# Every product as two of 64 stationary columns, in a linear-attention and expert kernel on one Trainium2 core

## The chip, the cores and the metric

The kernel runs on one core of one Trainium2 chip. The metric is the device time of one execution in microseconds (us). All data are float32. "TensorE" (PE in the profile) multiplies matrices, "PEld" is its loading of weights (the stationary operand), VectorE is DVE, ScalarE is ACT, GpSimd is POOL, and SyncE (SP) issues most of the DMAs.

## The reference

A layer norm, then linear attention with a decay per head and a gate, and beside it a linear layer with eight low-rank experts of which each token uses two; both are added to the input.

```python
BATCH, SEQ, HIDDEN = (2, 512, 512); HEADS, HEAD_DIM = (32, 128)
xn = layernorm(x)
qkv = silu(xn @ qkv_w.T)                       # 3 * 32 heads * 128
...                                             # per head, in blocks, with decay:
scores = einsum('bhnd,bhmd->bhnm', cq, ck) * diag_decay
intra  = einsum('bhnm,bhmd->bhnd', scores, cv)
inter  = einsum('bhnd,bhde->bhne', cq * q_decay, kv)
kv_next = kv * block_decay + einsum('bhnd,bhne->bhde', ck * k_decay, cv)
...
xf = attn * rsqrt(mean(attn * attn) + EPS)
gate = sigmoid(xn @ gate_w.T)
attn_out = gate * (norm_w * xf) @ out_w.T
...
probs = softmax(xn @ W_router.T); top 2 of 8, renormalised -> combine
h  = einsum('nd,erd->ner', xn, A) * combine[:, :, None]
ffn_out = xn @ W_base.T + b_base + einsum('ner,eor->no', h, B) * 2
return x + attn_out + ffn_out
```

## The kernel before

**Products.** A product is one call of `nc.tensor.matmul(o, lhsT, rhs)`: `lhsT` is the stationary operand (128 rows by up to 128 columns), `rhs` the moving one (128 rows by N columns), `o` a tile in PSUM with as many partitions as `lhsT` has columns. In float32 the compiler makes of each call two weight loads and two matrix instructions, one after the other: load, matmul, load, matmul. N is 256 in the projections, in the base linear layer and in the output projection, 128 in the attention, 512 in the experts' product and 136 in the router's. The code makes 3048 products: 2072 with N = 256, 936 with N = 128 (40 of them are products of the identity by itself, which fill two banks, and transposes), 32 with N = 136 and 8 with N = 512.

**Stages.** (1) The tokens (8 tiles of 128) are normalised, transposed on TensorE (`transpose`, L264) and used by the router's product (`router`, through `mm`, L90) and by the base linear layer (`base`, L314), which is split by a scheme of Strassen's kind into seven products of half size; the base product is spread among the transposes by hand (`AFTER`). (2) The projections to q, k, v and the gates: two levels of the same scheme, so 49 small products instead of 64. GpSimd makes the sums of weights (`encode`: tiles `s` and `e`), VectorE the sums of tokens (`xsum`, `xt`), and `inner_product` (L431 and L434) makes the products into banks named `ps_fr`, `ps_sc` and `sd`. ScalarE and VectorE combine the results (`after`: L503, L506, L519, L521, L527, L538). (3) The attention of one head and batch (`attend`): scores (`ps_sc<-qk`), state updates (`ps_sc<-v,kd`) and results (`ps_at`), all through `mm` (L90). k is brought into another layout by DMA through HBM (`k_kept`, `kt`). Its steps are placed among the slots of the projection loop. (4) The output projection, 16 pairs of heads for each of two halves of the tokens, again by seven products (`out_product`, L806), with sums made by VectorE (`gsum`) and GpSimd (`wsum`).

**Order.** From the transposes to the first output products the order on every engine is that of the code (`tc.manual_schedule`); one loop over slots of one inner product each (`SLOTS`, `later`, `stages`) interleaves projections, attention and DMAs. The rest of the output projection, after `in_order.close()` (L965), is ordered by the framework's scheduler. Accumulation: most products write with `start` on the first use of a bank only and with `skip_group_check=True`, so one bank holds several running sums.

`mm` (L89) is the helper through which the router, the attention and the experts go; `base`, `inner_product` and `out_product` call `nc.tensor.matmul` themselves.

Of the kernel before, what the change touches and what calls it, by code (L numbers as in the profile page):

```python
# [42 lines left out]
P = 128  # L43
# [7 lines left out]
NP = H // 2  # L51
# [10 lines left out]
def attn_moe_kernel(ctx: ExitStack, tc: tile.TileContext, x, qk_w, v_w, gate_w, out_w, norm_w,  # L62
                    decay, base_w, base_b, router_a_w, lora_b, out):
    nc = tc.nc
# [15 lines left out]
    def bank(tag):  # L80
        return ps.tile([P, 512], F32, tag=tag, name=f"ps_{tag}", bufs=banks[tag])
# [3 lines left out]
    def ring(tag, shape=None):  # L85
        n, bufs = RING[tag]
        return work.tile(shape or [P, n * 512], F32, tag=tag, name=tag, bufs=bufs)

    def mm(o, lhsT, rhs, start, stop):  # L89
        nc.tensor.matmul(o, lhsT, rhs, start=start, stop=stop)  # L90

    ssq = [keep.tile([P, S], F32, tag=f"ssq{b}", name=f"ssq{b}") for b in range(B)]
    ident = keep.tile([P, P], F32, tag="ident", name="ident")
# [18 lines left out]
    def inv_sqrt(mean_sq, y, z):  # L112

        nc.vector.reciprocal(y, z)
        nc.vector.scalar_tensor_tensor(z, mean_sq, EPS, y, ALU.add, ALU.mult)
        nc.vector.scalar_tensor_tensor(z, z, -0.5, y, ALU.mult, ALU.mult)
        nc.vector.scalar_tensor_tensor(y, z, 1.5, y, ALU.add, ALU.mult)
        return y
# [10 lines left out]
    def kind(n):  # L129
        return 2 if n >= VG else n % 2  # L130
# [60 lines left out]
    for n in range(NSET):  # L191

        start = {0: [(0, 1), (1, 1), (0, 6)], 1: [(0, 4), (1, 6)]}.get(n, [(n, 1), (n - 1, 4), (n, 6)])
# [11 lines left out]
    with tc.tile_pool(name="setup", bufs=1, side="right") as sp:  # L205
# [26 lines left out]
        def tokens(t, c):  # L232

            b, tt = divmod(t, TB)
            of = slice(tt * P, (tt + 1) * P)
            return xnT[:, c, of] if b == 0 else b12[:, c, of] if c < 2 else b22[:, c - 2, of]
# [8 lines left out]
        def statistics(t):  # L245
            if t:
                nc.vector.bn_stats(stats[:, t, :], x_sb[t])
                nc.vector.bn_aggr(mv[:, t, :], stats[:, t, :])
            else:
                both = sp.tile([P, 2, 6], F32, tag="both", name="both")  # L250
                for i, of in enumerate(halves):
                    nc.vector.bn_stats(both[:, i, :], x_sb[0][:, of])
                nc.vector.bn_aggr(mv[:, 0, :], both)
            for g, ts in enumerate(groups):
                if t == ts[-1]:
                    roots[g] = root(sp, mv[:, ts[0] : t + 1, 1], len(ts), f"ln{g}")
# [15 lines left out]
        def router(t):  # L272
            ra = bank("sc")
            for c in range(KC):
                mm(ra[:, : NE + ER], tokens(t, c), wra[:, c, :], c == 0, c == KC - 1)
            nc.scalar.copy(ra_sb[:, t, :], ra[:, : NE + ER])
# [3 lines left out]
        HO = HID // 2  # L280
# [3 lines left out]
        wo = dict(zip(range(1, 8), (a11, a12, wsums[3], a22, wsums[0], wsums[1], wsums[2])))  # L284
        xo = dict(zip(range(1, 8), (b11, b21, b22, xsum[3], xsum[0], xsum[1], xsum[2])))

        def base():

            pa, pb = seeded[:2], first_banks
            pc, pd, y, w = {}, {}, {}, {}  # L290

            def done(b, half, h, o):
                nc.sync.dma_start(x_base[:, TB * b + 2 * h : TB * b + 2 * h + 2, half * HO : (half + 1) * HO],
                                  o.rearrange("p (t n) -> p t n", t=2))

            def copied(tag, t):
                o = ring(tag, [P, 512])
                nc.scalar.copy(o, t)
                return o

            def added(t, u):
                o = ring("scores")
                nc.vector.tensor_tensor(o, t, u, ALU.add)
                return o


            units = [(1, 0, 0), (1, 0, 1), (2, 0, 0), (2, 0, 1), (1, 1, 0), (1, 1, 1), (2, 1, 0), (2, 1, 1)]
            for q, h, i in units + [(q, h, i) for q in (5, 6, 7, 3, 4) for h in range(2) for i in range(2)]:
                if q == 5 and i == 0:
                    pc[h] = bank("sc")  # L310
                t = {1: pa, 2: pa, 5: pc, 3: pc, 6: pb, 7: pd, 4: pd}[q][h]
                of = slice((2 * h + i) * P, (2 * h + i + 1) * P)
                for c in range(2):
                    nc.tensor.matmul(t[:, i * HO : (i + 1) * HO], xo[q][:, c, of], wo[q][:, c, :],  # L314
                                     start=q in (1, 5) and i == 0 and c == 0, stop=True, skip_group_check=True)
                if i == 0:
                    pass
                elif q == 1:
                    nc.scalar.copy(pb[h], t)
                elif q == 2:  # L320
                    done(0, 0, h, copied("scores", t))
                elif q == 5:
                    y[h] = copied("gT", t)
                elif q == 6:
                    pd[h] = pa[h]
                    nc.scalar.copy(pd[h], t)
                    w[h] = copied("gate", t)
                elif q == 7:
                    done(1, 1, h, added(t, y[h]))
                elif q == 3:  # L330
                    done(1, 0, h, added(t, w[h]))
                else:
                    done(0, 1, h, copied("scores", t))
                yield

        chunks = base()

        first_banks = [seeded[2], bank("at")]  # L340
# [10 lines left out]
        for g, ts in enumerate(groups):  # L351
            rstd = inv_sqrt(*roots[g])
            xns = []
            for i, t in enumerate(ts):
                xn = ring("gate")
                for of in halves if t == 0 else (slice(0, HID),):
                    (nc.vector if t < NT - 1 else nc.gpsimd).tensor_scalar(
                        xn[:, of], x_sb[t][:, of], mv[:, t, 0:1], rstd[:, i : i + 1], ALU.subtract, ALU.mult)
                xns.append(xn)

            for t in range(2 * g, 2 * g + 2) if 0 < g < 4 else ():
                statistics(t)
            for t, xn in zip(ts, xns):
                transpose(t, xn)
                for what in AFTER[t]:
                    if what == "base":
                        next(chunks)
                    else:
                        router(what)
        nc.vector.tensor_tensor(wsums[0], a21, a22, ALU.add)  # L370
        nc.vector.tensor_tensor(wsums[1], wsums[0], a11, ALU.subtract)
        nc.vector.tensor_tensor(wsums[2], a11, a21, ALU.subtract)
# [15 lines left out]
        HB = S // 2  # L388
# [34 lines left out]
    def inner_product(o, r, i, first):  # L423
        n, q = rounds[r]
        a = operand[n, q][i]
        x_ = {1: xo[q][:, 0, :HB], 2: xo[q][:, 1, :HB], 3: xo[q][:, 1, HB:], 4: xt[q - 1][:, 3],
              5: xt[q - 1][:, 0], 6: xt[q - 1][:, 1], 7: xt[q - 1][:, 2]}[i]
        for u in range(2):
            if kind(n) == 0:

                nc.tensor.matmul(o.rearrange("p (g j d) -> p j g d", g=2, j=2)[:, u], x_[:, u * P : (u + 1) * P],  # L431
                                 a, start=first and u == 0, stop=True, skip_group_check=True)
            else:
                nc.tensor.matmul(o[:, u * HB : (u + 1) * HB], a[:, u], x_, start=first and u == 0, stop=True,  # L434
                                 skip_group_check=True)

# [215 lines left out]
    def attend(head, b):  # L654
# [22 lines left out]
        for j in range(TB):  # L677
            mm(pc[:, j * P : (j + 1) * P], k[:, j * P : (j + 1) * P], q[:, j * P : (j + 1) * P], True, True)
# [77 lines left out]
    HT, HO = S // 2, HID // 2  # L756
# [37 lines left out]
    def out_product(f, p, n, sums, only=None):  # L794

        a, w = gated[f, p], w_o[p]
        o = sums[n] if isinstance(sums[n], list) else [sums[n][:, i * HO : (i + 1) * HO] for i in range(2)]
        if n in (1, 2):
            l, r = a[:, n - 1, 0], w[:, n - 1, :HO]
        else:  # L800
            s, t = gsum[f, p], wsum[f, p]
            l, r = {3: (s[:, 3], w[:, 1, HO:]), 4: (a[:, 1, 1], t[:, 3]), 5: (s[:, 0], t[:, 0]),
                    6: (s[:, 1], t[:, 1]), 7: (s[:, 2], t[:, 2])}[n]
        for i in range(2):
            if only in (None, i):
                nc.tensor.matmul(o[i], l[:, i * P : (i + 1) * P], r,  # L806
                                 start=p == 0 and (i == 0 or isinstance(sums[n], list)), stop=p == NP - 1, skip_group_check=True)

    EARLY = 4
    sums = [{}, {}]  # L810
# [36 lines left out]
    for k in range(7 * len(rounds) + 7):  # L847
        now[0] = k
        r0, m = divmod(k, 7)
        if m == 0:  # L850
# [10 lines left out]
            if r0 < len(rounds):  # L861
                n, q = rounds[r0]
                state_of[r0] = {}
                for _, to in ADDED[q]:
                    if to == "u3":
                        outer_sums[n, to] = outer_sums[n, "u2"]
                    elif isinstance(to, str):
                        if (n, q) == (1, 1):

                            t = [ring("qk", [P, 2, 512]) for _ in range(2)]  # L870
                            outer_sums[n, to] = [t[ij // 2][:, ij % 2] for ij in range(4)]
                        else:
                            t = aw2.tile([P, 4, 512], F32, tag="sum", name="sum", bufs=3)
# [22 lines left out]
        back, i = SLOTS[m]  # L896
        r = r0 - back
# [218 lines left out]
```

## Time and profile before

| | |
|---|---|
| median of 3 runs | 1130.0 us (1128.63 to 1130.0) |
| span of the profiled execution | 1129.5 us, granted TensorE clock 1.000 |
| PE busy / PEld busy | 1120.4 us (99%) / 1004.9 us (89%), 6064 instructions recorded for each |
| DVE / ACT / POOL busy | 755.1 (67%) / 433.9 (38%) / 763.5 us (68%) |
| DMA | 198.24 MB, mean 176 GB/s |
| instruction fetch (queue q8) | 0.80 MB in 49 packets, 0.3% of the DMA engines' time |

The profiled execution has no time of its own beside its span; the span lies 0.5 us under the median of the runs and within their spread. In the lines of the profile, a group of instructions is given by line, engine, operation, "out<-in" by the program's names, shape and count, then the busy time and the mean length of one, then the idle time of the engine before them with what ended it. The timeline gives start and length in us, engine, line, operation and count of merged neighbours. Lengths of matmuls are modelled and overlap; what an instruction costs is read from start to start. L90 and the like are lines of the kernel before.

### The profile page before, as it was taken

The numbers are of one execution on the slowest core, as the hardware profiler recorded it, in microseconds if no ns is written. First come the engines' busy times: TensorE is split into PE (matmuls) and PEld (weight loads), VectorE is DVE, ScalarE is ACT, GpSimd is POOL, SyncE is SP. The second block draws the span as 40 slices with busy tenths as digits, with TensorE's granted clock in tenths as the row PEclk, the third lists the DMA queues.
The fourth block names the chain that finished last, engine by engine and source line by source line (L and its number), as shares of the span: only waits on it lengthen the run. The fifth ranks groups of instructions, "written<-read, shape, count | busy, mean of one in ns | idle before, by whom it ended". The sixth has DMA issues, their size and how long they took to land.

```text
span 1129.5 us, 18355 instructions
## 1 busy us (share of the span) xinstructions
PE 1120.4 (99%) x6064; PEld 1004.9 (89%) x6064; DVE 755.1 (67%) x1343; ACT 433.9 (38%) x778; POOL 763.5 (68%) x819
## 2 busy tenths in 40 slices
PE   8999999999999999999999999999999999999998
PEld 8888888888888888998999999999999998888887
DVE  7676766675665667776767767677777775545424
ACT  4344444444435434343343444435344442320000
POOL 3568778779768767666686866768776666554552
PEclk9999999999999999999999999999999999999999
DMA  5534574664553456666665766766666677943221
GB/s 169 161 112 158 168 235 157 193 203 156 186 168 122 159 146 198 168 195 187 208 193 173 209 170 179 204 190 198 179 186 174 200 229 242 329 162 118 90 92 56
DMA packets 192254, 198.24 MB, mean 176 GB/s; under 512 B 50976, under 2 KB 164384, under 8 KB 192032
## 3 DMA queue, kind: packets, MB, share of 16 engines
q1 hardware_dynamic: 192016, 196.94, 56.9%
q8 instruction: 49, 0.80, 0.3%
q14 instruction: 45, 0.37, 0.1%
q10 hardware_dynamic: 144, 0.13, 0.0%
HBM read 126.70 MB, written 70.30 MB: 174 GB/s over the span
## 4 chain that ended last, share of the span: by engine, by line
PE 93%; DMA 3%; DVE 2%; SPq 1%; issue 1%; POOL 1%; ACT 0%; ACTq 0%; DVEq 0%; POOLq 0%
PE ps_fr L434 20%; PE sd L434 18%; PE ps_at L90 9%; PE ps_sc L90 9%; PE sd L431 6%; PE sd L806 6%; PE ps_sc L806 5%; PE ps_fr L806 5%; PE ps_sc L434 4%; PE ps_sc L431 4%; PE ps_fr L431 4%; DMA k_kept<-squares 2%; PE ps_at L806 1%; PE sd L314 1%; DMA kt<-k_kept 1%; PE ps_sc L314 1%
## 5 line engine op out<-in xcount | busy, mean ns | idle before, releaser
L718 POOL TENSOR_TENSOR ssq<-ssq,sq 128x512 f32<-128x512 f32 x62 | 78.9, 1273 | 146.9 <-ACT sq L717 146.9
L434 PE MATMUL sd<-xt,e 128*128 128x256 f32 x672 | 172.6, 379 | 0.0
L483 ACT ACTIVATE qk<-qk 128x512 f32<-128x512 f32 x128 | 80.4, 630 | 207.0 <-DVE qk L506 206.9
L434 PEld LDWEIGHTS sd<-xt,e 128*128 128x128 f32 x672 | 123.6, 190 | 17.2 <-issue 2.6
L538 ACT COPY sd<-sd 128x512 f32<-128x512 f32 x112 | 64.1, 573 | 137.9 <-PE sd L434 69.3
L521 DVE TENSOR_TENSOR w<-sd,sum 128x512 f32<-128x512 f32 x110 | 74.5, 690 | 63.1 <-ACT sd L538 62.9
L527 ACT COPY sd<-ps_fr 128x512 f32<-128x512 f32 x112 | 64.2, 573 | 77.3 <-PE ps_fr L434 49.2
L90 PE MATMUL ps_at<-scores,v 128*128 128x128 f32 x512 | 88.4, 275 | 0.0
L787 POOL TENSOR_TENSOR wsum<-wo 128x256 f32<-128x256 f32 x48 | 39.2, 834 | 68.2 <-PE sd L806 28.9
L90 PEld LDWEIGHTS ps_at<-scores,v 128*128 128x128 f32 x512 | 77.4, 191 | 3.4
L786 DVE TENSOR_TENSOR gsum<-gated 128x256 f32<-128x256 f32 x54 | 25.9, 520 | 80.7 <-PE ps_sc L806 56.6
L162 POOL TENSOR_TENSOR s<-raw 128x1024 f32<-128x1024 f32 x32 | 75.6, 2364 | 5.0 <-DMA raw<-in_v_w 2.9
L90 PE MATMUL ps_at<-qd,state 128*128 128x128 f32 x384 | 74.2, 275 | 0.0
L434 PE MATMUL ps_fr<-xsum,s 128*128 128x256 f32 x288 | 74.0, 379 | 0.0
L710 DVE SCALAR_TENSOR_TENSOR gT<-gate,ps_at 128x512 f32<-128x512 f32 x64 | 43.6, 682 | 41.9 <-PE ps_at L90 36.8
L90 PEld LDWEIGHTS ps_sc<-qk 128*128 128x128 f32 x512 | 67.2, 192 | 3.3
L90 PE MATMUL ps_sc<-qk 128*128 128x128 f32 x512 | 67.5, 275 | 0.0
L181 POOL TENSOR_TENSOR e<-s 128x256 f32<-128x256 f32 x64 | 46.6, 728 | 28.7 <-PE sd L434 18.0
L683 POOL TENSOR_TENSOR qd<-qk,mask 128x384 f32<-128x384 f32 x64 | 64.3, 1005 | 2.4 <-PE ps_at L90 2.0
L680 DVE TENSOR_TENSOR scores<-ps_sc,mask 128x512 f32<-128x512 f32 x64 | 43.9, 686 | 22.4 <-PE ps_sc L90 20.0
L434 PEld LDWEIGHTS ps_fr<-xsum,s 128*128 128x128 f32 x288 | 53.1, 190 | 6.4
L90 PEld LDWEIGHTS ps_sc<-v,kd 128*128 128x128 f32 x384 | 52.6, 191 | 6.8 <-ACT kd L690 3.7
(345 smaller groups left out, 2905.8 us busy)
## 6 DMA issues: line engine op xcount, KB each, us to landing
raw<-in_qk_w SPq DMA_DIRECT2D x64, 256.0 KB, 4.3
v<-v_kept SPq DMA_DIRECT2D x64, 256.0 KB, 4.4
gate<-gate_kept SPq DMA_DIRECT2D x64, 256.0 KB, 3.3
g_kept<-gT SPq DMA_DIRECT2D x64, 256.0 KB, 3.3
gated<-g_kept SPq DMA_DIRECT2D x27, 512.0 KB, 3.8
k_kept<-squares SPq DMA_DIRECT2D x64, 192.0 KB, 3.5
kt<-k_kept SPq DMA_DIRECT2D x256, 48.0 KB, 2.1
gate_kept<-v SPq DMA_DIRECT2D x47, 256.0 KB, 2.5
```

The costliest lines, as they stand in the source:

```text
L90: nc.tensor.matmul(o, lhsT, rhs, start=start, stop=stop)
L162: nc.gpsimd.tensor_tensor(t, a, b, op)
L181: nc.gpsimd.tensor_tensor(e[:, 0], a21, a22, ALU.add)
L431: nc.tensor.matmul(o.rearrange("p (g j d) -> p j g d", g=2, j=2)[:, u], x_[:, u * P : (u + 1) * P], a, start=first and u == 0, stop=True, ...
L434: nc.tensor.matmul(o[:, u * HB : (u + 1) * HB], a[:, u], x_, start=first and u == 0, stop=True, skip_group_check=True)
L483: nc.scalar.activation(v, v, AF.Silu)
L521: nc.vector.tensor_tensor(o, v, t, ALU.add)
L527: nc.scalar.copy(st["pb"], st["pa"])
L538: nc.scalar.copy(st["pd"], st["pb"])
L683: nc.gpsimd.tensor_tensor(qd, q[:, P:].rearrange("p (j n) -> p j n", j=TB - 1), mask[:, 1, :].unsqueeze(1).to_broadcast([P, TB - 1, P]), A ...
L718: nc.gpsimd.tensor_tensor(ssq[b], ssq[b], sq, ALU.add)
L806: nc.tensor.matmul(o[i], l[:, i * P : (i + 1) * P], r, start=p == 0 and (i == 0 or isinstance(sums[n], list)), stop=p == NP - 1, skip_grou ...
```

## The change

A flag, `in_halves`, is false at first and is set after the last transpose of the tokens has been written. From there on `mm` makes of each product two: one with the stationary columns 0 to 63, whose result is partitions 0 to 63 of the bank, and one with columns 64 to 127 and partitions 64 to 127. Each has the whole moving operand. The program that is built states a tile of 128 rows by 64 columns at column 0 or 64 of the array for them. `base`, `inner_product` and `out_product` now call `mm` as well. The flag is set when part of the base product has been written; of the 3048 products, 88 stay whole (the identities, the transposes, the router's and 16 of the base's) and 2960 become 5920: 4112 with N = 256, 1792 with N = 128, 16 with N = 512. The two halves of a product follow each other in TensorE's order. The semaphore that tells other engines of a finished bank is raised after the second half.

```diff
-    def mm(o, lhsT, rhs, start, stop):
-        nc.tensor.matmul(o, lhsT, rhs, start=start, stop=stop)
+    HP = P // 2
+    in_halves = [False]
+
+    def mm(o, lhsT, rhs, start, stop, **more):
+
+        if not in_halves[0]:
+            nc.tensor.matmul(o, lhsT, rhs, start=start, stop=stop, **more)
+            return
+        for h in range(2):
+            of = slice(h * HP, (h + 1) * HP)
+            nc.tensor.matmul(o[of], lhsT[:, of], rhs, start=start, stop=stop, **more)
...
-                    nc.tensor.matmul(t[:, i * HO : (i + 1) * HO], xo[q][:, c, of], wo[q][:, c, :],
-                                     start=q in (1, 5) and i == 0 and c == 0, stop=True, skip_group_check=True)
+                    mm(t[:, i * HO : (i + 1) * HO], xo[q][:, c, of], wo[q][:, c, :],
+                       q in (1, 5) and i == 0 and c == 0, True, skip_group_check=True)
...
+        in_halves[0] = True
         nc.vector.tensor_tensor(wsums[0], a21, a22, ALU.add)
...
-                nc.tensor.matmul(o.rearrange("p (g j d) -> p j g d", g=2, j=2)[:, u], x_[:, u * P : (u + 1) * P],
-                                 a, start=first and u == 0, stop=True, skip_group_check=True)
+                mm(o.rearrange("p (g j d) -> p j g d", g=2, j=2)[:, u], x_[:, u * P : (u + 1) * P], a,
+                   first and u == 0, True, skip_group_check=True)
             else:
-                nc.tensor.matmul(o[:, u * HB : (u + 1) * HB], a[:, u], x_, start=first and u == 0, stop=True,
-                                 skip_group_check=True)
+                mm(o[:, u * HB : (u + 1) * HB], a[:, u], x_, first and u == 0, True, skip_group_check=True)
...
-                nc.tensor.matmul(o[i], l[:, i * P : (i + 1) * P], r,
-                                 start=p == 0 and (i == 0 or isinstance(sums[n], list)), stop=p == NP - 1, skip_group_check=True)
+                mm(o[i], l[:, i * P : (i + 1) * P], r, p == 0 and (i == 0 or isinstance(sums[n], list)), p == NP - 1,
+                   skip_group_check=True)
```

## Prediction

> **What bounds the kernel now.** I read the page's busy times first, then its slices, then the chain that ended last, and then the timeline of TensorE in three short windows, because a busy share alone does not say what an instruction costs.
>
> ```profile
> PE 1120.4 (99%) x6064; PEld 1004.9 (89%) x6064; DVE 755.1 (67%) x1343; ACT 433.9 (38%) x778; POOL 763.5 (68%) x819
> PEclk9999999999999999999999999999999999999999
> PE 93%; DMA 3%; DVE 2%; SPq 1%; issue 1%; POOL 1%; ACT 0%; ACTq 0%; DVEq 0%; POOLq 0%
> ```
>
> TensorE works 1120.4 of 1129.5 us at the full clock (mean granted 1.000) and holds 93% of the chain. VectorE and GpSimd are busy two thirds of the time: if TensorE gets slower, nobody else becomes late. Every product of the source is two matrix instructions (6064 recorded for 3048 products in the code; a few records are missing), each with its own weight load. So the cost of an edit here is the change in the start-to-start time of TensorE's instructions, times their number. The timeline gives those times (start, length, engine, line, operation, count):
>
> ```profile
> 400.54 1.03 PE L434 MATMUL ps_fr<-xnT,raw 128*128 128x256 f32 x4
> 401.40 1.03 PE L434 MATMUL ps_fr<-xt,e 128*128 128x256 f32 x4
> 402.26 1.03 PE L434 MATMUL sd<-xt,e 128*128 128x256 f32 x4
> ```
>
> ```profile
> 498.12 0.39 PE L90 MATMUL ps_at<-qd,state 128*128 128x128 f32 x2
> 498.34 0.39 PE L90 MATMUL ps_at<-scores,v 128*128 128x128 f32 x2
> 498.57 0.39 PE L90 MATMUL ps_at<-qd,state 128*128 128x128 f32 x2
> ```
>
> Four instructions (two products) of 256 moving columns start 0.86 us apart from the next four: 216 ns per instruction, 432 per product. Two of 128 columns start 0.224 us apart (median over the trace 112 each): 224 per product. The lengths that the groups print (379 and 275 ns) are longer than these steps because instructions overlap; they are not prices.
>
> What a weight load costs when nothing hides it is seen only where TensorE had run dry:
>
> ```profile
> 87.93 1.03 PE L431 MATMUL sd<-e,xt 128*128 128x256 f32 x4
> 89.15 1.13 PE L431 MATMUL ps_sc<-e,xsum 128*128 128x256 f32 x4 [0.19 <-DVE y L521]
> ```
>
> ```profile
> 445.33 0.94 PE L90 MATMUL ps_sc<-v,kd 128*128 128x128 f32 x6 [0.58 <-ACT kd L690]
> ```
>
> The same group of four takes 1.03 us in the stream and 1.13 after a wait. In the single records, the first instruction after a wait is followed by the second 320 ns later instead of 216, and by 213 to 214 instead of 112 at 128 columns; the second weight load starts 107 ns after the first. So 128 columns of weights take 107 ns when exposed, the pure stream is 320 - 107 = 213 ns (256 columns) or 107 (128), and in the steady stream the load is hidden: of 6063 loads, 6028 begin 1 to 5 ns after the matmul before them in the list has begun, and none earlier.
>
> Check of the model: in the trace 4143 starts at 216 and 1840 at 112 make 895 + 206 = 1101 us; with 9 us of 136 columns, 7 of 512 and 11 us by which stalls exceed these steps it is 1128, the span within 1.5. The span of 1129.5 is 0.5 under the median of the runs (1130.0, from 1128.63), so sums on the span stand for the time.
>
> **The change part by part.** *What is untouched.* The start-up and the first part of the base product, 88 of 3048 products, keep the full width. On all engines but TensorE the same instructions stand in the same order up to the tail, where a handful of the last combines, weight sums and loads change place; the loads are issued tens of us ahead of need, so I cost that at nothing. If it were not covered, one late load costs what the longest such wait shows, some 8 us.
>
> *What is doubled.* 2960 products become two each: 2056 with 256 columns, 896 with 128, 8 with 512. TensorE's list afterwards goes, for one product, load, matmul, load, matmul on the lower half (its two passes), then the same on the upper half; halves alternate through the whole list with two exceptions. Each matmul still streams all its moving columns, so per product there are four streams instead of two. They cost the same time as before only if the second pass of one half runs beside the first pass of the other. The trace has no instruction on part of the array, so this must be bounded.
>
> *Lower bound.* Halves run fully beside each other and every load is hidden: a product costs two pure streams, 2 x 213 = 426 (-6) or 2 x 107 = 214 (-10). That is -6 x 2056 - 10 x 896 = -12 - 9 = -21 us: 1109.
>
> *Upper bound.* No overlap: four steps of 216 or 112 a product, +432 x 2056 + 224 x 896 + 858 x 8 = 888 + 201 + 7 = +1096 us: 2226 (2180 with pure streams).
>
> *The value I take* follows from the order in which the trace shows TensorE to work: a load starts only once the matmul before it in the list has started. With halves, the matmul in the way is the second pass of the lower half, which cannot start before the first pass has streamed. Only then can the weights of the upper half be loaded, and its first pass begins one load later, beside the running one. The same is repeated when the list returns to the lower half. So a product costs two streams plus two exposed loads. Half the columns I put at half of 107, 53.5 ns (bounds 0 and 107, as all loads in the trace have 128 columns). Then: 2 x (213 + 53.5) = 533 against 432, +101 x 2056 = 208 us; 2 x (107 + 53.5) = 321 against 224, +97 x 896 = 87 us; 961 against 858 for the eight, 1 us. Sum +296. The 11 us of stalls shrink as TensorE falls behind its suppliers; say 4 go. 1130 + 296 - 4 = about 1422. With the ends of the load, 0 gives 1109 and 107 gives 640 and 428 a product, +428 + 183 + 2: 1743.
>
> The Trainium skill (TensorE: Matmul & The Clock Gate, Part 3, What overlaps and what doesn't) says that a weight load overlaps running matmuls only where its row group differs. Here loads on the same rows overlap all the time (89% load beside 99% matmul), so as it stands the trace contradicts it for a full-width array; for halves no run shows it, and if it held for them the loads would be exposed as in my forecast at least.
>
> *Small terms.* The signal that a bank is full moves to the upper half's last pass: consumers start at most one stream and one load (0.27 us) later per product. The combining engines wait that out with a third of their time free; uncovered, it would matter only in the chain of small steps of one head, where other products stand between. Instruction fetching doubles for TensorE; it moves 0.80 MB now in 0.3% of the queues' time, cover enough.
>
> **The rivals.** *Both halves free (faster).* Mechanism: each half has its own place for coming weights and a load may pass a matmul that waits for the other half. Then the loads vanish and the 21 us of the lower bound are gained at most: 1109 to 1127, middle 1117. It decides as soon as an upper-half load starts before the lower half's second pass does. For it: 128-column steps are 112 where the stream is 107, so hidden loads do cost a little now. Against it: no load in the trace ever begins before the matmul ahead of it. If the gain is eaten by a few ns per added instruction, the time is unchanged (within 0.2%, about 2 us, which is all that a measurement of this kernel can tell). The Trainium skill (TensorEngine Tiling, Key Properties) sides with this rival: tiles run loads and matmuls in parallel. No run here shows it; by it the sum would be the lower bound.
>
> *Issue-bound.* Halves overlap, but TensorE must now start four load-matmul pairs per product. The trace shows pairs no closer than about 109 ns, with the stream as the likely reason. If a pair costs c to issue, a 128-column product costs 4c: it decides from c = 56 ns there, from 108 at 256 columns. At the most that rows allow, c = 112: +224 x 896 + 16 x 2056 = 201 + 33 us: 1364. Half-way 1240. For it: the added instructions are real; against it: nothing shows a pair to be slow.
>
> *No overlap at all.* The change then doesn't do what it says and costs the upper bound, about 2200. For it: matmuls start strictly in list order. Against it: the two halves write different partitions and the list alternates between them.
>
> **How the numbers follow.** Exposed loads 0.37 (about 1422, own range 1330 to 1600); issue-bound 0.22 (1135 to 1364); free halves 0.18 (1109 to 1127) and unchanged 0.04; no overlap 0.19 (2180 to 2226). The range leaves only the last out, so it reaches from 1108 to 1600. Faster by over 0.2%: 0.18, within 0.04, slower 0.37 + 0.22 + 0.19 = 0.78.
>
> **What would show it.** In the timeline after, the two halves' matmuls should come as pairs a load apart: first pass upper 50 ns after second pass lower, and 530 ns from product to product at 256 columns, 320 at 128, in line with each other (+100 each). Issue-bound would show 128-column products as slow as 256-column ones; free halves would show 426 to 432 with two starts within a few ns; no overlap 860 and evenly spaced starts. Idle time of VectorE and GpSimd should rise with the span, all of it waiting for TensorE; if instead TensorE waits for them, or the granted clock falls below 1.0, the prediction is wrong in its reasons.

## The result and the profile after

The changed kernel takes 1135.27 us (median of 20 runs, 1128.34 to 1143.04) against 1129.19 us before (median of 20, 1127.87 to 1131.8): ratio 1.0057, interval 1.0041 to 1.0072. It is slower by 6 us, not by 292, and its runs lie nearly four times as far apart (14.7 us from lowest to highest, for 3.9). The profiled execution (1142.24 us, span 1140.5, mean granted clock 0.995) is the second longest of the 20; what follows accounts for its 11.0 us over the span of before, of which the median run has about half.

The page after: span, busy times, two of its DMA queues (packets, MB, share of the engines' time), the chain by engine, and the DMA issue of k's first leg (count, KB each, median us to landing).

```profile
span 1140.5 us, 30213 instructions
PE 1122.3 (98%) x11984; PEld 863.1 (76%) x11984; DVE 753.8 (66%) x1343; ACT 434.2 (38%) x778; POOL 764.3 (67%) x819
q1 hardware_dynamic: 192016, 196.94, 55.3%
q8 instruction: 95, 1.56, 0.6%
PE 89%; DMA 6%; DVE 2%; SPq 2%; issue 1%; ACT 1%; POOL 1%; ACTq 0%; DVEq 0%; POOLq 0%
k_kept<-squares SPq DMA_DIRECT2D x64, 192.0 KB, 4.2
```

Nearly twice the recorded matrix instructions, and TensorE is busy hardly longer (1122.3 for 1120.4 us). Its busy share falls because it waits: 18.2 us idle for 9.1. In the chain DMA has gone from 3% to 6% and SyncE's queue from 1% to 2%; the median landing of `k_kept` went from 3.5 to 4.2 us.

The timeline of TensorE in the stretches that the prediction read (start, length, engine, line, shape, count; L99 is the halved product in `mm`):

```profile
400.41 1.06 PE L99 MATMUL ps_fr<-xnT,raw 128*64 128x256 f32 x8
401.27 1.06 PE L99 MATMUL ps_fr<-xt,e 128*64 128x256 f32 x8
402.13 1.06 PE L99 MATMUL sd<-xt,e 128*64 128x256 f32 x8
```

```profile
498.45 0.39 PE L99 MATMUL ps_at<-qd,state 128*64 128x128 f32 x4
498.66 0.39 PE L99 MATMUL ps_at<-scores,v 128*64 128x128 f32 x4
498.88 0.39 PE L99 MATMUL ps_at<-qd,state 128*64 128x128 f32 x4
```

Eight half instructions now start 0.86 us apart from the next eight, where four whole ones did; four of 128 columns take 0.21 to 0.22 us, where two took 0.224. In the single records the half instructions come in pairs whose two starts lie 7 ns apart (in most others 21 or 36), and pairs follow each other every 216 ns at N = 256 and every 109 ns at N = 128. So two streams run side by side. The records give the width of a matmul, not its half; that a pair is one matmul of each half is read from the order of the code and from the run `four_four` below.

Where the time went is seen when the span is cut at the same places of the work: start and length of the stretch, busy time (instructions) of PE, PEld, DVE, ACT, POOL, granted clock, DMA share, GB/s. First before, then after:

```profile
0.00:408.00 408.00, 404.48 (x1889) 352.61 (x1890) 280.02 (x464) 181.97 (x336) 298.60 (x321) 1.00 0.52 166
408.00:949.00 541.00, 538.66 (x3356) 496.62 (x3356) 390.99 (x719) 226.54 (x404) 374.63 (x384) 1.00 0.66 193
949.00:1130.00 181.00, 177.22 (x822) 155.66 (x820) 84.06 (x162) 25.39 (x39) 90.31 (x115) 1.00 0.43 144
```

```profile
0.00:408.00 408.00, 404.89 (x3636) 309.47 (x3638) 281.22 (x464) 182.28 (x336) 299.21 (x321) 1.00 0.51 167
408.00:960.00 552.00, 540.20 (x6714) 424.36 (x6712) 390.05 (x721) 226.94 (x405) 375.45 (x384) 0.99 0.64 190
960.00:1141.00 181.00, 177.19 (x1641) 129.22 (x1636) 82.50 (x161) 25.00 (x39) 89.60 (x115) 1.00 0.43 145
```

The first 408 us and the last 181 are the same. All the 11 us are lost in the middle, where attention is placed among the projections: TensorE idles 11.8 us there for 2.3 (+9.5) and is busy 1.5 us longer, at a granted clock of 0.99.

TensorE's waits by what ended them (us in total, times, longest), before and then after, name the first of two losses:

```profile
PE ps_sc L90 <- ACT kd L690: 2.2, 3, 0.9
```

```profile
PE ps_sc L99 <- ACT kd L699: 11.6, 6, 2.4
```

The wait is that of the state products for `kd`, k in its other layout. k goes by way of a transposition on VectorE, `k_kept` to HBM, `kt` back in four pieces, and ScalarE's scaling. The attention runs 64 times, once for each head and batch; over the eight of these with the least room (every eighth, from the fourth on) the transposition's end to the issue of `k_kept` takes 0.56 us on average before and 2.02 after, the issue of `k_kept` to that of the first `kt` 4.70 and 5.38, the whole way to `kd` 9.77 and 11.4. So most of the delay is there before `k_kept` is issued. SyncE issues in order, and its own longest waits for a transfer, before and after, show where it stands meanwhile:

```profile
SPq L673 <- DMA k_kept<-squares: 77.1, 49, 3.8
```

```profile
SPq L682 <- DMA k_kept<-squares: 99.7, 52, 4.6
```

To issue `kt` it waits until `k_kept` of one item has landed, and the `k_kept` of the next item stands behind that. Late issues and long transfers go together: of the 64 transfers of `k_kept`, 41 are issued within 0.1 us of the transposition's end before and 23 after. Those take 2.7 and 3.2 us from issue to their last packet, the others 3.9 us in both kernels.

The clock is the second part of the loss. The timeline at the longest wait shows the wait in brackets, and the stretch after it the clock (the columns are those of the stretches above):

```profile
716.10 1.03 PE L99 MATMUL ps_fr<-xsum,raw 128*64 128x256 f32 x8
719.50 1.36 PE L99 MATMUL ps_sc<-v,kd 128*64 128x128 f32 x12 [2.37 <-ACT kd L699]
720.64 1.93 PE L99 MATMUL sd<-xt,e 128*64 128x256 f32 x8
```

```profile
720.00:723.00 3.00, 3.00 (x21) 2.09 (x20) 0.87 (x3) 0.34 (x1) 0.03 (x1) 0.50 0.86 243
```

After a wait that cost 2.75 us start to start, TensorE runs at half its clock: eight half instructions that took 1.06 us take 1.93. Such stretches of 3.4 us begin at 719.7, 791.4 and 951.9 us, 0.2 to 1.1 us after the end of a wait of 2.5 to 2.75 us start to start; the waits of 1.75 to 2.1 us (446, 514 and 583) were not followed by one. The length of the wait alone does not decide it. The times at which the clock changes lie whole multiples of 3.413 us apart (21 and 47 of them between these three). With the 16 traces of this case cut into steps at these places, nine steps of their bodies have TensorE without a matmul for 2.00 to 3.03 us, and each is followed by a step at half clock; in every other step it is idle for at most 1.93 us, and none of those is. So a wait that straddles two steps can be longer and cost no clock. One of 2.45 us in `spread46` (below), which lies 0.80 us in one step and 1.65 in the next, is followed by full speed:

```profile
792.78 0.94 PE L90 MATMUL ps_sc<-v,kd 128*128 128x128 f32 x6 [2.45 <-ACT kd L690]
793.55 1.03 PE L434 MATMUL sd<-xt,e 128*128 128x256 f32 x4
```

Each stretch at half clock costs about 1.7 us, 5 in all. Before, there is none in the body of the kernel. The 5 us are more than the 1.5 by which TensorE's busy time grew: by that the streams themselves became some 3.5 us shorter (an estimate).

### The profile page after: what moved, and what is told of

The parts are those of the page before. It is cut to its first block, busy times and chain, and to the rows that moved or that the text cites. A ratio compares the mean times of both kernels' runs of the same rounds, so it can differ in the third digit from the quotient of the medians.

```text
span 1140.5 us, 30213 instructions
## 1 busy us (share of the span) xinstructions
PE 1122.3 (98%) x11984; PEld 863.1 (76%) x11984; DVE 753.8 (66%) x1343; ACT 434.2 (38%) x778; POOL 764.3 (67%) x819
## 3 DMA queue, kind: packets, MB, share of 16 engines
q1 hardware_dynamic: 192016, 196.94, 55.3%
## 4 chain that ended last, share of the span: by engine, by line
PE 89%; DMA 6%; DVE 2%; SPq 2%; issue 1%; ACT 1%; POOL 1%; ACTq 0%; DVEq 0%; POOLq 0%
PE sd L99 30%; PE ps_fr L99 27%; PE ps_sc L99 21%; PE ps_at L99 9%; DMA k_kept<-squares 3%; DMA kt<-k_kept 1%; SPq L682 1%; PE ps_sc L95 1%; PE sd L95 1%; DMA mask<-in_decay 1%; PE ps_fr L273 0%; POOL s L171 0%; DVE qk L515 0%; ACT kd L699 0%; DMA x<-in_x 0%
## 5 line engine op out<-in xcount | busy, mean ns | idle before, releaser
L99 PE MATMUL sd<-xt,e 128*64 128x256 f32 x1344 | 176.5, 381 | 0.0
L99 PEld LDWEIGHTS sd<-xt,e 128*64 128x64 f32 x1344 | 101.4, 138 | 37.4 <-issue 2.9
L99 PE MATMUL ps_at<-scores,v 128*64 128x128 f32 x1024 | 90.0, 276 | 0.0
L99 PE MATMUL ps_at<-qd,state 128*64 128x128 f32 x768 | 75.1, 274 | 0.0
L99 PE MATMUL ps_fr<-xsum,s 128*64 128x256 f32 x576 | 75.1, 379 | 0.0
L99 PEld LDWEIGHTS ps_at<-scores,v 128*64 128x64 f32 x1024 | 65.9, 139 | 9.8 <-issue 0.7
L99 PEld LDWEIGHTS ps_sc<-qk 128*64 128x64 f32 x1024 | 60.4, 137 | 9.1
L99 PE MATMUL ps_sc<-qk 128*64 128x128 f32 x1024 | 66.8, 273 | 0.0
L99 PE MATMUL ps_sc<-v,kd 128*64 128x128 f32 x768 | 53.7, 275 | 11.6 <-ACT kd L699 11.6
L99 PEld LDWEIGHTS ps_sc<-v,kd 128*64 128x64 f32 x768 | 46.0, 138 | 23.2 <-ACT kd L699 15.3
L99 PE MATMUL sd<-e,xt 128*64 128x256 f32 x448 | 59.1, 379 | 0.0
```

The lines of the kernel that those rows point to most:

```text
L99: nc.tensor.matmul(o[of], lhsT[:, of], rhs, start=start, stop=stop, **more)
```

## The experiments

The ratios are to the kernel before, run beside each on the same chip. "Waits for `kd`" is the sum of the view of waits above (2.2 us before, 11.6 after).

**Halves in one sort of product only.** What does a halved product cost among whole ones, and are the projections or the attention at fault?

```diff
+    def rhs_wide(rhs):
+        return int(np.prod(rhs.shape[1:])) > P
-        if not in_halves[0]:
+        if not in_halves[0] or rhs_wide(rhs):        # attn_only
+        if not in_halves[0] or not rhs_wide(rhs):    # wide_only
```

> Only products of 128 moving columns (the attention's 896) go as halves; those of 256 and 512 stay whole. TensorE's list then changes between whole-width and half-width tiles some 380 times and has 3584 instructions more instead of 11840. Theory 1 (instruction fetch: the streams of the halves are free, and the loss of the change comes from fetching twice the instructions, which makes the k transposition's DMAs late): 128-column steps fall from 112 to 109 ns, which is 5 us less; some 14 more instruction packets instead of 46, so few of the new waits: 1125 to 1129 us if changing the tile is free. If each change of the tile drains the array (one exposed load of 107 ns to one empty pipe of about 170 ns), 40 to 65 us more: 1165 to 1195. Theory 2 (the second stream's reads disturb the DMAs): a fifth of the extra reading, also 1125 to 1129 without drains. Theory 3 (the faster attention only runs into its own supplies): 1129 to 1131, the waits before the state products (ps_sc<-v,kd) grow by what the attention gains.

> The other part: only products of 256 and 512 moving columns go as halves, the attention's stay whole. 8256 instructions more, some 32 instruction packets. Theory 1: no step gets faster (216 ns before and after), so nothing is gained, and the waits before the state products come with most of the fetch: 1131 to 1136 plus the price of changing the tile found in attn_only. Theory 2: four fifths of the extra reading, the same 1131 to 1136. Theory 3: the attention is as slow as before, so 1129 to 1130 (plus the tile changes).

Measured: `attn_only` 1190.26 us, ratio 1.0531 (1.0517 to 1.0546); `wide_only` 1194.85, ratio 1.0570 (1.0556 to 1.0584). Both lose ten times what the whole change loses. The change of width costs so much here that the two runs cannot tell the theories of their expectations apart (their waits for `kd` are gone). The timeline of `attn_only` (L98 whole, L102 halved) and its waits of weight loads show where:

```profile
500.20 1.03 PE L98 MATMUL ps_fr<-b,s 128*128 128x256 f32 x4
501.15 1.09 PE L102 MATMUL ps_sc<-qk 128*64 128x128 f32 x16
502.18 1.13 PE L98 MATMUL sd<-xt,e 128*128 128x256 f32 x4
```

```profile
PEld ps_sc L102 <- issue: 31.2, 94, 0.3
PEld ps_at L102 <- issue: 21.2, 64, 0.3
```

At most changes of the width the loads wait for nothing that the profile shows. There are 192 steps from whole to half (309 ns start to start instead of 216) and 192 back (202 instead of about 102), and what follows is late too (160 ns to the next pair instead of 109, and 320 to the next whole matmul instead of 216). `attn_only` lost 60 us although attention itself gains nearly 5 (the two kernels differ by 4.6): 65 over 384 changes is 0.17 us a change, and the four delays just named add up to the same; `wide_only` lost 64. The changed kernel makes this change of width once, so it pays next to nothing for it. The Trainium skill (TensorEngine Tiling, Key Properties) says that changing the tiling mode drains TensorE. These two runs agree in so far as every change costs 0.17 us; the records show late starts, not the drain itself.

**Both lower halves, then both upper ones.** The two products of a projection slot are listed with both lower halves before both upper halves, so that a strictly ordered engine would run two products on one half before the other starts.

```diff
+    def mm(o, lhsT, rhs, start, stop, halves=(0, 1), **more):
...
+        for h in halves:
...
-        for u in range(2):
+        for h, u in ((0, 0), (0, 1), (1, 0), (1, 1)):
...
-                mm(o[:, u * HB : (u + 1) * HB], a[:, u], x_, first and u == 0, True, skip_group_check=True)
+                mm(o[:, u * HB : (u + 1) * HB], a[:, u], x_, first and u == 0, True, (h,), skip_group_check=True)
```

> All products as halves, but in the inner products of the projections the lower halves of both products come first and then both upper halves: four matmuls on the lower half of the array, then four on the upper. If matmuls start strictly in list order, the upper four can only begin with the last of the lower four: six steps per pair of products instead of four, 1568 products of the projections, +1568 x 0.216 = 340 us, about 1475 us. If matmuls of one half pass those that wait for the other half (theory of how the halves got free), and the window is at least four deep: as the changed kernel, 1131 to 1140. With a window of one or two matmuls: between, 1200 to 1400.

Measured 1140.69 us (1127.54 to 1144.95), ratio 1.0080 (1.0055 to 1.0105). The timeline of its TensorE:

```profile
450.48 1.09 PE L99 MATMUL ps_sc<-qk 128*64 128x128 f32 x16
451.35 1.08 PE L99 MATMUL ps_fr<-xt,e 128*64 128x256 f32 x8
452.22 1.08 PE L99 MATMUL sd<-xt,e 128*64 128x256 f32 x8
```

Still eight half instructions in 0.87 us. The two starts of a pair are now mostly 57 to 59 ns apart, about one half load. Strict order would have cost some 340 us (the estimate of the expectation). By the order of the list, then, the upper half's first pass starts ahead of three matmuls that stand before it: TensorE looks at least four matmuls ahead and lets one pass others that wait for the other half. The order in the list costs nothing in the streams here; the waits for `kd` are 12.0 us, as in the changed kernel.

**Is it the instruction fetch?** The added instructions come in 46 more packets of 16 KB (95 for 49), which take 1.07 us each on average. In the kernel before, 46 small transfers were added, at regular places of the middle, from ScalarE's queue: 23 KB on a single DMA engine (`one_engine46`), 32 KB spread over sixteen (`spread46`), or in the same places two copies of 128x160 on ScalarE without any transfer (`act46`).

```diff
         now[0] = k
+        if k >= 14 and k % 17 == 0:
+            extra = dram.tile([23, 512], F32, tag=f"extra{k}", name="extra")   # 32 rows in spread46
+            nc.scalar.dma_start(extra[:, :256], x[0:23, :256])
```

```diff
+        if k >= 14 and k % 17 == 0:
+            for _ in range(2):
+                nc.scalar.copy(spare_row, nw_row)      # act46
```

> The kernel before, all products whole, with 46 small DMAs added that are issued by ScalarE's queue, each of 23 packets of 1 KB (HBM to HBM, about 1 us) on one single DMA engine, spread over the projection loop: the load that 46 more instruction packets put on the DMA engines, without more instructions and without halves. What they copy is not used. Theory 1: the k transposition's DMAs become late now and then, waits before the state products grow as in the changed kernel: 1131 to 1137. Theories 2 and 3: nothing but 46 issues on ScalarE, 1129 to 1130.

> Control to one_engine46: the kernel before with the same 46 issues on ScalarE's queue at the same places, 32 packets of 1 KB instead of 23, but spread over 16 DMA engines, two packets (about 0.1 us) on each. If what delayed the way of k in one_engine46 (+18 us) is one DMA engine held for about a microsecond, as an instruction packet of 16 KB holds one: little is left, 1130 to 1134. If it is the issues on ScalarE or the bytes: again 1143 to 1149.

> The kernel before with two short ScalarE copies (128x160, some 0.3 us each) at the 46 places at which one_engine46 and spread46 issue a DMA, and no DMA: it holds ScalarE as long as the issues do (0.50 to 0.57 us). If those two kernels were slow because ScalarE was late (+13 us in both), this one is too: 1140 to 1146, and what one held DMA engine costs is only the 5 us between them. If it is the added transfers, even when spread: 1130 to 1133.

Measured: `one_engine46` 1148.14 us, ratio 1.0153 (1.0139 to 1.0167); `spread46` 1142.58, ratio 1.0117 (1.0096 to 1.0138); `act46` 1129.91, ratio 1.0000 (0.9991 to 1.0009). TensorE's waits in the first two:

```profile
PE ps_sc L90 <- ACT kd L690: 13.5, 7, 3.0
```

```profile
PE ps_sc L90 <- ACT kd L690: 10.9, 9, 2.4
```

Whole products and a few added small transfers bring the same wait, with the same half-clock stretches after it (three in `one_engine46`, one in `spread46`). `one_engine46` is 11 us above what was expected. The queue of the added transfers moves 1.21 and 1.64 MB (0.13 of it was there before), 0.3% and 0.6% of the DMA engines' time. Of my story that one engine held by a packet makes the transfer of `k_kept` late, little is left: spread over all engines the transfers cost nearly three quarters as much (12.9 of 17.8 us over the kernel before, 1129.72 and 1130.39 beside them). The packets themselves do not settle it: in the changed kernel the 13 transfers of `k_kept` that have a packet of instructions beside them in their first 2.5 us take 3.63 us to their last packet and the other 51 take 3.66, but in `after_k_at_2` (below) 14 take 3.41 and 50 take 2.72. ScalarE's time is not it either, since `act46` costs nothing and its list of waits has none for `kd`. So the way of k has hardly any room, and both kinds of small transfer, issued 46 times, make it late.

**Start k's way earlier.** If late k is the whole loss, the changed kernel with k in good time should beat the kernel before. First the transposition and `k_kept` went one slot earlier, the load of v behind them (`early_k`; in `early_k2` both lie in one slot), in the changed kernel and, as a control, in the kernel before.

```diff
-        v = ring("v")
-        nc.sync.dma_start(v, v_kept[s_][:, u, f, b, :])
-        yield
         squares = work.tile([P, 4, TB - 1, 32], F32, tag="squares", name="squares", bufs=2)
...
         nc.sync.dma_start(kept, squares)
         yield
+        v = ring("v")
+        nc.sync.dma_start(v, v_kept[s_][:, u, f, b, :])
+        yield
```

```diff
-        for slots in (1, 2, 3, 6):
+        for slots in (1, 1, 2, 6):      # early_k2 only, besides
```

> The changed kernel, with one edit in the attention: the transposition of k and its DMA to HBM (k_kept) come one slot of the loop earlier than now, and the load of v one or two slots later. The way of k (k_kept, kt, kd) gets about 1 us more before its product. Theory 1 (the halves' streams are free, the loss is waits for the k way, made late by instruction fetching, and the half-clock windows that follow such waits): the waits of 1.7 to 2.7 us shrink by about 1 us each and some windows go, 1128 to 1132. If the loss lies elsewhere (the streams themselves, the signal of the later half, other buffers): no change, 1135.

> The kernel before (whole width) with the edit of after_early_k. It has three such waits of about 1 us in its profile; they can go: 1127 to 1130. It tells how much of a gain in the two other kernels is the edit's own. Against it the gain of the halves by themselves should stand: 3 to 5 us between this and the best of the edited changed kernels.

> As after_early_k, but the k_kept DMA is issued one slot earlier still, in the slot of the transposition. About 2 us more for the way of k. Theory 1: nearly all new waits go and with them the half-clock windows; what is left is the gain of the 128-column steps (112 to 109 ns, 5 us): 1124 to 1128. If SyncE now waits for the transposition and holds up what is behind it, some of that is lost: up to 1131. If the loss lies elsewhere: 1135.

> The kernel before with the edit of after_early_k2: 1126 to 1130, as before_early_k, since few waits are left to remove.

Measured, changed kernel and control: 1134.16 and 1137.59 us (ratios 1.0034, interval 1.0023 to 1.0044, and 1.0055, 1.0040 to 1.0071); `early_k2` 1134.69 and 1137.53 (1.0036, 1.0025 to 1.0047, and 1.0057, 1.0042 to 1.0073). The controls miss their expectations (1127 to 1130 and 1126 to 1130), and the changed kernel comes close to the 1135 that was expected if the loss lay elsewhere. The waits for `kd` are gone or at most 0.6 us, but the transposition now stands ahead of other work of VectorE, and a combine on ScalarE is late instead. The view of waits of `before_early_k`:

```profile
PE ps_fr L434 <- ACT sd L527: 6.9, 8, 1.1
```

In the changed kernel this wait is 8.2 us in 9 times, in both forms of the edit. The edit is bad by itself, in both kernels. What it shows is the difference: with nearly the same wait in both, the halves are 3.4 and 2.8 us faster than whole products.

Then the transposition was left where it was, and only the issue of `k_kept` went from the third slot to the second, right behind it (`k_at_2`); besides, in `k_v`, the load of v went from the first slot to the third, out of the way of k.

```diff
-        v = ring("v")                                          # k_v only
-        nc.sync.dma_start(v, v_kept[s_][:, u, f, b, :])        # k_v only
...
         nc.vector.transpose(squares.rearrange("p c j d -> p j c d"), k[:, : (TB - 1) * P])
-        yield
         kept = dram.tile([P, 4, TB - 1, 32], F32, tag="k_kept", name="k_kept", bufs=3)
         nc.sync.dma_start(kept, squares)
         yield
+        v = ring("v")                                          # k_v; in k_at_2 v stays
+        nc.sync.dma_start(v, v_kept[s_][:, u, f, b, :])        # ahead, and this slot is empty
+        yield
```

> The changed kernel; only the issue of the k_kept DMA moves, from the third slot after its head's result to the second, right behind the transposition, which stays where it is (early_k had moved that too, and brought waits of TensorE for ScalarE's copies of 8 us in all). The way of k gets about 1 us. Theory 1: of the 13.4 us that TensorE waits before the state products in the changed kernel some 6 to 12 go, and the half-clock windows with them; nothing new comes. 1125 to 1130, under the kernel before by the gain of the 128-column steps (3.4 us was measured between the two kernels with early_k). If SyncE, now waiting for the transposition with the loads behind it, becomes late elsewhere: 1130 to 1135.

> The kernel before with the same edit: its 3 us of waits before the state products can go, 1127 to 1130. The difference to after_k_at_2 is what the halves are worth when the way of k is not late: 2 to 5 us.

> As after_k_at_2, and the load of v goes behind k_kept, to the third slot, so that SyncE has one thing less to do ahead of k. v is needed only with the state product, later than k. 1125 to 1129; if v comes late now, waits before the same products, 1130 to 1135.

> The kernel before with the edit of after_k_v (k_kept issued with the transposition, v behind it), as the control to after_k_v (1126.8): 1127.5 to 1130. If the halves are worth 2 us or more once k is in time, it lies that much over 1126.8; if the edit alone made the gain, it is at 1126 to 1127 too.

| | time | ratio (interval) | waits for `kd` in the view |
|---|---|---|---|
| after_k_at_2 | 1128.01 us | 0.9980 (0.9965 to 0.9994) | 4.4 us, 2 times |
| before_k_at_2 | 1128.84 us | 0.9985 (0.9973 to 0.9997) | none |
| after_k_v | 1126.79 us | 0.9968 (0.9957 to 0.9978) | 1.9 us, 2 times |
| before_k_v | 1129.14 us | 0.9995 (0.9984 to 1.0005) | 1.1 us, once |

With `k_at_2` the halves are only 0.8 us ahead, less than the 2 to 5 expected: two waits for `kd` are left in the changed kernel's profiled run, one of them followed by a stretch at half clock (at 581.0 us). `after_k_v` is faster than both kernels. Its page and its wait:

```profile
span 1125.3 us, 30219 instructions
PE 1116.1 (99%) x11984; PEld 860.7 (76%) x11984; DVE 753.1 (67%) x1343; ACT 434.0 (39%) x778; POOL 764.2 (68%) x819
```

```profile
PE ps_sc L99 <- ACT kd L697: 1.9, 2, 1.6
```

The clock is 1.000 in its whole body, and TensorE is busy 4.3 us less than before (1116.1 for 1120.4). One DMA moved by a slot, and one out of its way, turn the change from 0.6% slower to 0.3% faster; the same edit does nothing measurable for whole products. So the loss was k's lateness, and the clock that goes with it, and the halves alone are worth some 3 us (3.6 gained by `after_k_v` less 0.6 by its control, each against its own runs of the kernel before).

What stays open is why k became late at all. The 46 added packets of instructions are the only traffic that the change adds, and 46 transfers of like or twice the size had the like effect, but that the packets are the cause was not isolated: no run doubles the fetch alone. That other transfers take longer because of how the halves read their operands is spoken against by the queue of the data: 55.3% of 1140.5 us is 631 us, for 643 before.

## Why the prediction was right or wrong

**The step that failed** is the order rule under "The value I take": that a load starts only once the matmul before it in the list has started, so that two exposed half loads are paid per product (+296 us). It was read correctly from whole-width instructions (6028 of 6063 loads), where each matmul needs the same columns as the one before, and was carried over to halves, where it does not hold. A product costs 432 and 218 ns (two pairs of 216 and 109) in place of the 533 and 321 of the prediction, so the +208 us of the 256-column products measured 0 and the +87 us of the 128-column ones about -5. After the change, with loads and matmuls counted in the order of their starts, 11784 of 11840 halved loads begin before the matmul just ahead of them has begun; 11756 begin 1 to 5 ns after the matmul two places ahead, which in alternating pairs is the last one of their own half. The rule is thus kept within each half and not across them.

One place shows the whole mechanism, because TensorE had just waited there. The timeline of matmuls and that of loads:

```profile
514.51 0.88 PE L99 MATMUL ps_sc<-v,kd 128*64 128x128 f32 x12 [1.38 <-ACT kd L699]
```

```profile
514.51 0.63 PEld L99 LDWEIGHTS ps_sc<-v,kd 128*64 128x64 f32 x12 [1.83 <-ACT kd L699]
```

The list is lower first pass, lower second, upper first, upper second. In the single records the first two matmuls that start are 7 ns apart (.509 and .516), the next two loads begin 54 ns after the first of them (.563 and .569), and the next pair of matmuls begins at .669, 160 ns after it. The upper half's first pass does not wait for the lower half's second, which could not have streamed in 7 ns. And 160 less the pure stream of 107 is 53 ns: the half load that I had put at 53.5 is right, only it is not exposed in the stream.

**The rival "both halves free"** had the mechanism, with its signs: 216 ns a pair (432 a product) at N = 256 and 7 ns between starts. Its size was too large. It counted 6 ns a product at N = 256 that did not come (0 came) and 10 at N = 128, of which 6 came (224 to 218): 896 times 6 is 5 us, and 2.8 to 3.4 us is what the controls without late k show. By itself it would have been "faster", as `after_k_v` is.

The Trainium skill (TensorEngine Tiling, Key Properties) says that different tiles can load and multiply in parallel; this trace agrees, with 7 ns between the two starts of a pair. The Trainium skill (TensorE: Matmul & The Clock Gate, Part 3, What overlaps and what doesn't) says that matmuls start and end strictly in program order and that loads overlap running matmuls only where the row group differs. Here, with two column halves on the same rows, neither holds: going by the code's order, the third matmul of the list starts second, and 11784 loads begin before the matmul just ahead of them in order of starts.

**Why it is slower all the same** lies in what I costed at nothing: that "nobody else becomes late", and that instruction fetching has "cover enough". The first failed: in the eight tightest items k comes 9.8 us after its transposition before and 11.4 after, and TensorE waits for it. Whether the fetch is what makes it late is not shown. The busy shares were read well (VectorE and GpSimd are as busy as before), but a chain of small steps with two DMAs and a blocking queue is no engine, and has no busy share. The view of waits of before already had its line: three waits for `kd`, up to 0.9 us, so k was landing at the last moment. SyncE issues in order: where `kt` waits for the landing of `k_kept`, everything behind it waits too (77.1 us before, 99.7 after). The price was +11 us in the profiled run and +6 in the median, with the clock that the longer waits take away and net of what the streams gained. The one sign that the prediction named for this, that TensorE waits for others or the clock falls below 1.0, is what the profile shows: right direction, wrong reason.

**Right**: 88 whole products and 2960 halved; the same instructions on the other engines; the tail at the same time (177.2 us of PE for 177.2); no issue cost, since 11984 instructions keep the pace of 6064; and the time lies inside the range, close to its lower end. That, like the right direction, is luck: 1135 is the lower edge of the issue-bound rival, whose sign (128-column products as slow as 256-column ones) is not there, and what made the kernel slower was in no term of the sum. Two slips change nothing: four pure streams a product (4 x 213 and 4 x 107) add up to some 2183, not 2180; and no records are missing from the 6064, since the 32 transposes have one matrix instruction each (3048 x 2 - 32).

## What to carry to other kernels

Two halves of the array's columns ran side by side here and passed each other's waiting matmuls, so the split cost nothing in streams; but every switch between whole and half width cost 0.17 us, so switch once or not at all. An order rule read from a trace holds for the case that the trace has: ask what the instructions in it conflict over before carrying it to instructions that conflict over less. When the change itself turns out neutral, look for the chain of DMAs that lands last (waits below 1 us in the view of waits, a queue that blocks in order): its slack decided here, and one transfer issued a slot earlier was worth more (7 us, from 1135.27 to 1128.01) than the halves themselves (3 us).

## What the runs showed of the hardware

- The granted clock changes on a grid of 3.413 us. In the 16 traces, each of the nine steps of this grid with 2.00 us or more without a matmul was followed by a step at half clock, and none with 1.93 us or less; three such steps cost 5 us in the changed kernel.
- Changing between whole and half width: 93 ns on the first matmul into halves, 100 ns on the first one back, 0.17 us with the late starts behind it (384 changes, 65 us).
- In float32 a load of 64 columns takes 53 to 55 ns where 128 take 107, and two half matmuls of 128 moving columns step every 109 ns where a whole one takes 112.
- 46 transfers of 23 KB on one DMA engine, 0.3% of the DMA engines' time, made this kernel 17.8 us longer, because of one chain of DMAs without room; 46 pairs of copies on ScalarE in their place cost nothing.
